# A planned two-layer attention kernel: score banks counted free a little sooner, projections due on two slopes, and all due steps set anew

## The chip, the cores and the metric

The kernel runs on one core of one Trainium2 chip. The metric is the device time of one execution in microseconds. Before the change the median of three runs is 3295.56 us (3295.05 to 3298.42).

## The reference

The input is x, 8 images of 64 x 64 positions with 256 channels, in float32. Two layers follow each other.

Layer 0 projects to q and k (`qkv = x @ w_qkv + b_qkv`, and v is k). The first 128 channels attend inside horizontal windows of 8 x 64 positions, the other 128 inside vertical windows of 64 x 8; every window has 512 positions and 4 heads of 32 channels. A depthwise 3 x 3 convolution of hard_swish(v) is added, and the result goes through hard_swish and an output projection:

```
context = concat(ch, cv)                      # the two kinds of windows
context = hard_swish(context + depthwise3x3(hard_swish(v)) + dw_bias)
return context @ w_out + b_out
```

Layer 1 attends over all 4096 positions of an image with 32 channels: f, g, h are projections with spectrally normalized weights.

```
s = einsum('bnd,bmd->bnm', g, f); beta = softmax(s)
v = einsum('bnm,bmd->bnd', beta, h)
out = gamma * (v @ kv + bv) + x
```

## The kernel before, in words

**Steps.** All 8 images are one stream of 960 steps. A step is a group of score matmuls (s, for 128 keys by 512 queries in each of four row groups of the array), the exponentials of these on ScalarE (ACT, `p<-s`), and later a group of value matmuls (num) that multiply the exponentials into the sum of values. An image has three kinds of units: eight `h` units (horizontal windows) of 4 steps; eight `v` units (vertical windows) of 3 steps, of which the second and the third have three passes of scores instead of two (they share 8 slots of keys in unequal parts, PASSES); and two `l` units (the global attention of layer 1) of 32 steps each, called L0 and L1 below. The first `h` unit of the next image stands ahead of the `l` units of the current one, so that it covers the handover. In PE's program the order is scores of step n, then values of step n - 1, with other PE work before or behind the values.

**Banks.** The scores use three pairs of PSUM banks in turn (`pairs`, two pairs a step), one bank collects the values, and one bank alone (`ps_mm`, one buffer) takes everything else: the projections of q and k (`project`, pq), the projections to f, g (`project_fg`, pf) and h (`project_h`, phd), its transposition (`turn_h`, ph) and the row sums (`sums`). So the next of these can begin only when the one before has been evicted by ACT.

**Filler.** A projection is four pieces (`product_pieces`, HALVES and two halves of the contraction), each 16 matmuls of 128 x 256. There are four projections for each of 8 blocks i of an image: m = 0 and 2 give q and k of the horizontal windows ("near", evicted to qh and kh), m = 1 and 3 those of the vertical windows ("far", evicted to qv, and to kn and kv). Near projections of blocks 1 to 4 (INSIDE) and all far ones of the next image are due while the `l` units of the image before run; `inside_due` spreads them. The exponentials of `l` units are added up by VectorE (DVE, `acc_l`), but the last of four rows is added by DMAs that GpSimd (POOL) issues (`gather`, acc_l and row_l alternately). Convolution taps, hard_swish, normalization and transposes are DVE's and ACT's other work; `clip` and `join` work on a block each. Values of v units go through DRAM (`kt` is written to `kvia` and fetched to `vs` by SyncE's queue, SP).

**The planner.** The order of everything is worked out while the program is built, by the class Flow (lines 90 to 294). Every piece of work is a Task with its engine, an assumed length, what it needs, and a step at which it is due, all from DUE (lines 49 to 55) and the unit's own first step. `step` (line 231) places the scores, then urgent work, the held values of the step before, ACT's evictions (`fill_act`), filler on PE (`fill_pe`), DVE's work (`fill_dve`), and last what SP and POOL issue. It keeps a clock for each engine with its assumed durations. `banks` (line 162) says when the planner takes a pair of banks for free, as the end of the first exponential of the step before plus a lag less a fixed lead; `fill_pe` uses it as the time up to which filler is free, and `late` as the limit of what ACT may take on. A task whose due step has come is placed even if this delays the scores. `require` forces work that a step can't begin without. Since the engines then run in this order, each waits on the chip only for real dependences.

What the prediction's steps touch: `project` (L306 is the matmul's line in `product`), the evictions qh L634, qv L637, kh L649, kn L652 and kv L653, the clips L672 and L904, the first tap on ACT L704 and the other eight on DVE L708, the sums L859 and their copy L580, the copies of num L871 and L1052, `project_h` L956 with its eviction L964 and `turn_h` L970.

Of the kernel before, what the change touches and what calls it, by code (L numbers as in the profile page):

```python
# [21 lines left out]
TB = 512  # L22
NB = N // TB
# [17 lines left out]
def side(h):  # L41
    return slice(h * TB // 2, (h + 1) * TB // 2)
# [4 lines left out]
SLOTS = 8  # L47

DUE = dict(
    near_k=-4, near_q=0, near_values=-25, clip=0, swish=-2, conv_h0=51, conv_h1=13, conv_h2=38,  # L50
    conv_h3=23, conv_v0=-9, conv_v1=20, conv_v2=7, conv_v3=13, tap=-9, join_h=28, join_hl=17, join_v=-8,
    context=19, norm=3, release=-38, sums=8, add=-6, adds_h=1, adds_v=0, group_h=0, group_v=1, add2=-25,
    apart=6, fg0=-12, fg2=28, fg3=31, h0=3, h1=12, values_v=-33, near0=17, spread0=26, spread1=71,
    conv_first=0, far_swish=-33,
)
INSIDE = 4
AHEAD = 16
# [4 lines left out]
SCORES, VALUES, PROD, TURN, DRAIN, PASS, THIRD = 0.96, 0.88, 0.86, 0.65, 0.11, 0.43, 0.5  # L62
EXP, EVICT, COPY, VIEW = 0.97, 0.62, 0.52, 0.42
ADD, ADD3, NORM, SWISH, TAP, TAPS = 2.36, 1.83, 2.5, 0.75, 0.75, 1.28
GATHER, SUMMED = 0.9, 2.6
PE_LAG, LAG, SLACK = 0.28, 0.1, 0.3
ISSUE, LOAD, VIA, FETCH, HALO, BEHIND = 0.6, 4.3, 2.6, 2.8, 0.6, 3.0


# [20 lines left out]
class Flow:  # L90
# [70 lines left out]

    def banks(self):

        end = self.half_end + LAG - DRAIN
        return max(end, self.exp_end + LAG - DRAIN - THIRD) if self.third else end

    def late(self, end):
# [142 lines left out]
def tile_attention_blocks(  # L310
# [18 lines left out]
    nc = tc.nc  # L329
# [98 lines left out]
    sums = prep.tile([P, NF + C + 1], F32, name="sums")  # L428
# [31 lines left out]
    total = check.tile([1, 1], F32, name="total")  # L460
# [13 lines left out]
    def attention(images, load_x, out_rows, exact):  # L474
# [127 lines left out]
        def image(b):  # L602
# [136 lines left out]
            def window_unit(kind, i):  # L739
                nm = f"{b}_{'hv'[kind]}{i}"  # L740
                u = {}
                passes = PASSES if not exact and DUE["group_v" if kind else "group_h"] else {}
                adds = not exact and DUE["adds_v" if kind else "adds_h"]
                if passes:
                    terms = [(2, None)] if adds else [(2, None), ("mid", 1)]
                else:
                    terms = [(3, None)] if adds else [(2, None), (3, 0), (3, 1)]
                terms += [("acc", 0), ("acc", 1)]

                def maxima():  # L750
# [82 lines left out]
                def add(c):  # L833
# [2 lines left out]
                        u["acc"] = work.tile([P, NQ, TB], F32, tag="acc", name=f"acc_{nm}", bufs=1)  # L836
                    nc.vector.tensor_add(u["acc"], u["acc"] if c == 2 else u[0], u[c])  # L837

                def add_mid(c):

                    h = passes[c][0][1]
                    acc = u["acc"].rearrange("p (j i) c -> p i j c", j=2)[:, :, :, side(h)]
                    mid = u["mid", c].rearrange("p i (j c) -> p i j c", j=2)
                    nc.vector.tensor_add(acc, acc, mid)
# [61 lines left out]
                def context():  # L906
# [2 lines left out]
                    nc.vector.scalar_tensor_tensor(a, u["ctx"], 6.0, a, ALU.min, ALU.mult)  # L909

                return SimpleNamespace(
                    steps=3 if passes else 4, passes=passes, terms=terms, adds=adds,
                    scores=scores, weighted=weighted, add=add, add_mid=add_mid, sums=sums,
                    release=release, norm=norm, fetch=fetch, join=join,
                    clip=clip, context=context,
# [219 lines left out]
        flow = Flow()  # L1135
# [33 lines left out]
        readers, last_mids = defaultdict(list), {}  # L1169
# [13 lines left out]
        for u in units:  # L1183
            if not u.kind:
                continue
            e = u.t + u.steps
            w = [weights_ready(u.t + c) for c in range(u.steps)]
            if u.kind == "l":
                chain = None
                for c in range(1, u.steps):  # L1190
                    task = flow.add(
                        "dve", [(partial(u.add, c), [("dve", ADD if exact else ADD3)])], u.t + c + DUE["add"],
                        [w[c]] + ([w[0]] if c == 1 else [chain]), ready=u.t + c + 1,
                    )
                    if c == 1:
                        in_turn("acc", task)
                        readers[u.t].append(task)
                    readers[u.t + c].append(task)
                    chain = task
                gathered = []  # L1200
                for c in range(0 if exact else u.steps):
                    task = flow.add(
                        "rows", [(partial(u.gather, c), [("pool", GATHER), ("dma", SUMMED)])], u.t + c,
                        [w[c], *gathered[-2:-1]], ready=u.t + c + 1,
                    )
                    if c < 2:
                        task.after += last_users["acc"][-1:]
                    readers[u.t + c].append(task)
                    gathered.append(task)
                total = flow.add(  # L1210
                    "pe", [(u.sums, [("pe", PROD * (1 if exact else 1.5)), ("act", COPY)])], e + 1,
                    [chain, *gathered[-2:]], ready=e, bank=True,
                )
                in_turn("sum", total)
                last_users["acc"].append(total)
            else:
                pieces = [(partial(u.add, 1), [("dve", ADD)])]
                if u.passes:
                    pieces.append((partial(u.add_mid, 1), [("dve", TAPS)]))
                acc = pair = flow.add("dve", pieces, u.t + 2, w[:2], ready=u.t + 2)  # L1220
                in_turn("acc", acc)
                if u.adds:
                    add, took = (u.add_mid, TAPS) if u.passes else (u.add, ADD)
                    acc = flow.add(
                        "dve", [(partial(add, 2), [("dve", took)])], u.t + DUE["add2"],
                        [acc, w[2]], ready=u.t + 3,
                    )
                last = len(u.terms) - 1
                pieces = [
                    (  # L1230
                        partial(u.sums, n),
                        [("pe", PROD if h is None else PROD / 2), *([("act", COPY)] if n == last else [])],
                    )
                    for n, (_, h) in enumerate(u.terms)
                ]
                total = flow.add("pe", pieces, e, [acc, *w[2:]], ready=e, bank=True)
                total.then = (last, e + DUE["sums"])
                in_turn("sum", total)
                last_users["acc"].append(total)
                if u.passes:  # L1240
                    held = [(total, last)]
                else:
                    held = [acc if u.adds else (total, last), (total, 2)]
                first = (pair, 1) if u.passes else pair
                for c, task in enumerate((first, first, *held)):
                    readers[u.t + c].append(task)
                if u.passes:
                    last_mids[u.t + 1] = pair
                    last_mids[u.t + 2] = (total, 2) if acc is pair else acc
            u.released = flow.add("act", [(u.release, [("act", COPY)])], e + DUE["release"], ready=e)  # L1250
            shuffle = [("sp", ISSUE), ("dma", VIA)] if u.kind == "v" else []
            u.released.ends = True
            u.total = total
            u.normed = flow.add(
                "dve", [(u.norm, [("dve", NORM), *shuffle])], e + DUE["norm"], [total, u.released], ready=e
            )
            last_users["sum"].append(u.normed)
            u.fetched = u.normed
            if u.kind == "v":
                u.fetched = flow.add("sp", [(u.fetch, [("sp", 4 * ISSUE), ("dma", FETCH)])], e, [u.normed])  # L1260
# [27 lines left out]
        def inside_due(i, far):  # L1288

            n = i + min(i, INSIDE) + far  # L1290
            return DUE["spread0"] + (DUE["spread1"] - DUE["spread0"]) * n // (NB + INSIDE)

        for n, im in enumerate(ims):
            last = ims[n - 1] if n else None
# [3 lines left out]
            for i in range(NB):  # L1298
                u = h[i]
# [5 lines left out]
                ready = start if inside else last.v[0].t + DUE["near0"] if last else max(0, u.t - 4)  # L1305
                if i >= QH:
                    ready = max(ready, h[i - QH].t + u.steps)
# [15 lines left out]
                for m in (1, 3):  # L1323
                    after = [sw[i - 1, 1]] if m == 3 and i else []
                    ready, due = (start, start + inside_due(i, 1)) if last else (0, u.t + 1)
                    end = (("act", 2 * (VIEW if m == 1 else EVICT)),)
# [46 lines left out]
            context = {}  # L1373
# [85 lines left out]
        for u in units:  # L1459
            for c in range(u.steps if u.kind else 0):  # L1460
                n = u.t + c
# [46 lines left out]
        with tc.manual_schedule():  # L1508
            last = None
            steps = [(u, c) for u in units for c in range(u.steps)]  # L1510
            passes = [3 if u.kind in ("h", "v") and c in u.passes else 2 for u, c in steps] + [2]
# [93 lines left out]
```

## Time and profile before

| | |
|---|---|
| median of three runs | 3295.56 us |
| profiled execution | 3301.26 us, its span 3299.4 us |
| mean granted TensorE clock | 0.995 |
| PE busy | 98% of the span |
| DVE busy, ACT busy | 81%, 81% |
| POOL busy | 15% |
| exponentials of two-pass steps (L560) | 1664 of 1025 ns, 1612.6 us |
| adds of l units on DVE (L1037) | 480 of 1758 ns, 843.6 us |
| DMA, mean | 104 GB/s |

Each row of a group gives busy time, the mean of one instruction, and the idle time of the engine before it with what ended that. In a timeline the columns are the start in us, the length in us, engine, line, operation, tiles, shapes and count; `[... <- ...]` is the idle time before it and what released it. Lengths of merged rows reach from the first start to the last end. PE's matmuls overlap and their ends are modelled, so for PE the distance between the starts of neighbouring rows says more than the lengths. The first image takes about the first 300 us up to its `l` units, a middle image some 403 us, and the last image's `l` units, beside which no next image is projected, the last 200 us.

### The profile page before, as it was taken

Reading aid. Unit: us, or ns where it says so; the run is one execution under the profiler, and the core shown is the slowest. Engines: PE = TensorE matmul, PEld = TensorE weight load, DVE = VectorE, ACT = ScalarE, POOL = GpSimd, SP = SyncE. Lnnn points to the kernel's source line nnn. Section 1 sums busy time; section 2 is a strip of 40 time slices with the busy share of each in tenths; the row PEclk is TensorE's granted clock in tenths of the full one; section 3 lists DMA queues with packets and bytes.
Section 4 is the critical chain, followed back from the end, with each engine's and each line's share of the span. In section 5 each row is a group of like instructions: output and inputs, shape, how many; then the busy total and the mean of one; then the engine's idle time right before and its main releaser. Section 6 shows DMA issues by size and latency. Waiting matters only on the chain. (4 is left out here: it accounts for less than half of the span.)

```text
span 3299.4 us, 83480 instructions
## 1 busy us (share of the span) xinstructions
PE 3244.3 (98%) x35348; PEld 1182.5 (36%) x35348; DVE 2662.0 (81%) x2404; ACT 2663.4 (81%) x3235; POOL 510.8 (15%) x776
## 2 busy tenths in 40 slices
PE   7899999999999999999999999999999999999998
PEld 2344233432334323353333533334333342334422
DVE  4899688986899759997698976989769987689864
ACT  5688787887878878888788887788877888778876
POOL 0001230012200222002220022200321003210132
PEclk9999999999999999999999999999999999999999
DMA  2124652256523565235542365423654236532465
GB/s 73 48 83 117 124 123 91 77 127 125 110 91 86 122 130 112 82 87 123 128 107 80 101 119 125 103 78 104 124 130 100 78 101 130 125 102 65 104 128 110
DMA packets 321118, 344.41 MB, mean 104 GB/s; under 512 B 34272, under 2 KB 198624, under 8 KB 320736
## 3 DMA queue, kind: packets, MB, share of 16 engines
q0 software_dynamic: 71680, 134.25, 23.1%
q1 hardware_dynamic: 246816, 204.18, 20.8%
q8 instruction: 280, 4.59, 0.6%
q10 hardware_dynamic: 2240, 0.56, 0.1%
q14 instruction: 102, 0.84, 0.1%
HBM read 99.78 MB, written 83.89 MB: 56 GB/s over the span
## 5 line engine op out<-in xcount | busy, mean ns | idle before, releaser
L560 ACT ACTIVATE p<-s 128x1024 f32<-128x1024 f32 x1664 | 1612.6, 1025 | 226.7 <-PE s L1006 149.6
L1037 DVE TENSOR_TENSOR acc_l<-acc_l,p 128x1536 f32<-128x1536 f32 x480 | 843.6, 1758 | 350.6 <-ACT p L560 346.8
L708 DVE SCALAR_TENSOR_TENSOR act<-hv,dw_sb,act 128x1024 f32<-128x1024 f32 x512 | 653.0, 1279 | 18.0 <-ACT act L704 7.9
L1006 PE MATMUL s<-gq,f 32*128 32x512 f32 x4096 | 606.3, 640 | 4.3 <-ACT p L560 4.0
L306 PE MATMUL pq<-x,wqkv_sb 128*32 128x256 f32 x8192 | 540.3, 384 | 8.5 <-ACT kv L653 6.4
L1022 PE MATMUL num_l<-p,h_sb 128*32 128x512 f32 x4096 | 545.5, 605 | 0.3 <-ACT nums_l L1052 0.3
L306 PEld LDWEIGHTS pq<-x,wqkv_sb 128*32 128x32 f32 x8192 | 267.2, 111 | 393.1 <-issue 243.0
L799 PE MATMUL s<-qh,kh 32*128 32x512 f32 x2048 | 299.0, 640 | 6.4 <-ACT qh L634 5.6
L1048 POOL DMA_DIRECT2D row_l<-p x240 | 211.4, 881 | 507.6 <-ACT p L560 494.4
L828 PE MATMUL num_h<-p,vs 128*32 128x512 f32 x2048 | 273.3, 606 | 8.0 <-ACT nums_h L871 4.4
L1048 POOL DMA_DIRECT2D acc_l<-p x240 | 210.9, 879 | 426.0 <-ACT p L560 371.3
L1006 PEld LDWEIGHTS s<-gq,f 32*128 32x128 f32 x4096 | 173.6, 182 | 279.9 <-issue 264.0
L306 PE MATMUL s<-act,wout_sb 128*32 128x512 f32 x2048 | 227.6, 594 | 0.2 <-ACT ot_l L1115 0.2
L775 PE MATMUL s<-qv,kv 32*128 32x256 f32 x3072 | 218.8, 397 | 0.2 <-ACT p L793 0.2
L1022 PEld LDWEIGHTS num_l<-p,h_sb 128*32 128x32 f32 x4096 | 80.7, 108 | 384.3 <-issue 371.3
L1088 ACT ACTIVATE ot_l<-s,bias_o 128x512 f32<-128x512 f32 x120 | 76.2, 684 | 163.3 <-PE s L306 152.1
L821 PE MATMUL num_v<-p,vs 128*32 128x256 f32 x3072 | 194.0, 386 | 0.0
L775 PEld LDWEIGHTS s<-qv,kv 32*128 32x128 f32 x3072 | 146.5, 185 | 81.6 <-issue 57.9
L788 ACT ACTIVATE p<-s 128x1024 f32<-128x1024 f32 x128 | 131.5, 1027 | 44.0 <-PE s L775 44.0
L687 POOL MEMSET hv<- 128x18 f32 x64 | 20.6, 322 | 924.0 <-ACT sum_sb_v L580 712.5
L837 DVE TENSOR_TENSOR acc_v<-p 128x2048 f32<-128x2048 f32 x64 | 146.5, 2288 | 17.6 <-PE sum_h L859 7.8
L837 DVE TENSOR_TENSOR acc_h<-p 128x2048 f32<-128x2048 f32 x64 | 145.9, 2279 | 14.0 <-ACT p L560 12.8
(140 smaller groups left out, 3197.6 us busy)
## 6 DMA issues: line engine op xcount, KB each, us to landing
acc_l<-p POOLq DMA_DIRECT2D x256, 256.0 KB, 3.4
row_l<-p POOLq DMA_DIRECT2D x256, 256.0 KB, 3.3
x<-in_xT SPq DMA_DIRECT2D x92, 512.0 KB, 4.1
kvia<-kt SPq DMA_DIRECT2D x128, 256.0 KB, 2.5
vs<-kvia SPq DMA_DIRECT2D x512, 64.0 KB, 2.0
out<-ot_l SPq DMA_DIRECT2D x128, 256.0 KB, 2.1
via_v<-nums_v SPq DMA_DIRECT2D x64, 256.0 KB, 2.0
shuf_v<-via_v SPq DMA_DIRECT2D x256, 64.0 KB, 2.1
```

Source lines behind the costliest of these rows:

```text
L306: nc.tensor.matmul(out[quad(r), :], lhsT=lhsT[:, quad(r)], rhs=rhs, start=start, stop=stop)
L560: nc.scalar.activation(pt[:, 2 * z : 2 * z + 2, :], sc[z], AF.Exp, scale=scale)
L708: nc.vector.scalar_tensor_tensor(o, src, wt, o, ALU.mult, ALU.add)
L775: mm = nc.tensor.matmul(place_of(n, r, h, sc), lhsT=k[quad(r), t * P : (t + 1) * P], rhs=q[quad(r), side(h)], start=True, stop=True,)
L799: nc.tensor.matmul(row_of(sc, r), lhsT=k[quad(r), c * P : (c + 1) * P], rhs=q[quad(r), :], start=True, stop=not exact,)
L821: nc.tensor.matmul(u["num"][quad(r), side(h)], lhsT=vs[kind, i][:, r, t, :], rhs=place_of(n, r, h, (pt[:, :2], u["mid", c], pt[:, 2:])), s ...
L828: nc.tensor.matmul(u["num"][quad(r), :], lhsT=vs[kind, i][:, r, c, :], rhs=u[c][:, r, :], start=(c == 0), stop=(c == 3),)
L837: nc.vector.tensor_add(u["acc"], u["acc"] if c == 2 else u[0], u[c])
L1006: nc.tensor.matmul(row_of(sc, r), lhsT=f4[quad(r), c * P : (c + 1) * P], rhs=gq[quad(r), z, :], start=True, stop=not exact,)
L1022: nc.tensor.matmul(u["num"][quad(r), :], lhsT=h_sb[:, c, :], rhs=u[c][:, r, :], start=(c == 0), stop=(c == 4 * NB - 1),)
L1037: nc.vector.tensor_add(acc, u[0][:, :rows, :] if c == 1 else acc, u[c][:, :rows, :])
L1048: nc.gpsimd.dma_start(out=u["row", c % 2], in_=u[c][:, rows, :], accum_op=ALU.add)
```

## The change

It has four parts.

1. `banks` counts the score banks free 0.16 us sooner (the new constant EARLY).
2. `inside_due` goes through three points, spread0, spread_mid and spread1, instead of through two: one slope up to the blocks INSIDE, another from there on.
3. All due steps in DUE are other numbers; spread_mid and add3 are new.
4. Further adds of exponentials on DVE in place of row-sum matmuls can be asked for (`extra`, `add_more`); how many are made is set by adds_h and adds_v, which stay at 1 and 0.

```diff
 DUE = dict(
-    near_k=-4, near_q=0, near_values=-25, clip=0, swish=-2, conv_h0=51, conv_h1=13, conv_h2=38,
-    conv_h3=23, conv_v0=-9, conv_v1=20, conv_v2=7, conv_v3=13, tap=-9, join_h=28, join_hl=17, join_v=-8,
-    context=19, norm=3, release=-38, sums=8, add=-6, adds_h=1, adds_v=0, group_h=0, group_v=1, add2=-25,
-    apart=6, fg0=-12, fg2=28, fg3=31, h0=3, h1=12, values_v=-33, near0=17, spread0=26, spread1=71,
-    conv_first=0, far_swish=-33,
+    near_k=-7, near_q=-2, near_values=-50, clip=42, swish=21, conv_h0=106, conv_h1=18, conv_h2=27,
+    conv_h3=36, conv_v0=65, conv_v1=13, conv_v2=32, conv_v3=27, tap=-21, join_h=-53, join_hl=28,
+    join_v=12, context=-28, norm=14, release=-34, sums=-18, add=48, adds_h=1, adds_v=0, group_h=0,
+    group_v=1, add2=12, add3=98, apart=8, fg0=-7, fg2=-15, fg3=3, h0=36, h1=7, values_v=-102, near0=-69,
+    spread0=14, spread1=66, spread_mid=68, conv_first=80, far_swish=-20,
 )
...
-PE_LAG, LAG, SLACK = 0.28, 0.1, 0.3
+PE_LAG, LAG, SLACK, EARLY = 0.28, 0.1, 0.3, 0.16
...
-        end = self.half_end + LAG - DRAIN
+        end = self.half_end + LAG - DRAIN - EARLY
...
-                if passes:
-                    terms = [(2, None)] if adds else [(2, None), ("mid", 1)]
-                else:
-                    terms = [(3, None)] if adds else [(2, None), (3, 0), (3, 1)]
+                last = 2 if passes else 3
+                extra = [("mid", 2) if passes else ("all", 2), (0, last), (1, last)][:adds]
+                terms = [(last, None), (last, 1), ()][max(0, adds - 1)]
+                terms = [terms] if terms else []
+                if not adds:
+                    terms = [(2, None), ("mid", 1)] if passes else [(2, None), (3, 0), (3, 1)]
...
+                def add_more(what, c):
+
+                    if what == "mid":
+                        return add_mid(c)
+                    cols = slice(0, TB) if what == "all" else side(what)
+                    acc = u["acc"][:, :, cols]
+                    nc.vector.tensor_add(acc, acc, u[c][:, :, cols])
...
-            return DUE["spread0"] + (DUE["spread1"] - DUE["spread0"]) * n // (NB + INSIDE)
+            first, mid, last = DUE["spread0"], DUE["spread_mid"], DUE["spread1"]
+            if n <= 2 * INSIDE + 1:
+                return first + (mid - first) * n // (2 * INSIDE + 1)
+            return mid + (last - mid) * (n - 2 * INSIDE - 1) // (NB - INSIDE - 1)
```

The tasks that call `add_more` replace the one that called `add` or `add_mid` for the third step of a unit, and the lists of readers that free the slots of the exponentials name them.

More of the change, by code (lines that the diff above doesn't have):

```diff
@@ L911, in window_unit @@
                 return SimpleNamespace(
-                    steps=3 if passes else 4, passes=passes, terms=terms, adds=adds,
+                    steps=3 if passes else 4, passes=passes, terms=terms, extra=extra, add_more=add_more,
                     scores=scores, weighted=weighted, add=add, add_mid=add_mid, sums=sums,
@@ L1221, in attention @@
                 in_turn("acc", acc)
[L1222 to L1226, printed above, removed]
+                mores = {}
+                for what, c in u.extra:
+                    acc = mores[what] = flow.add(
+                        "dve", [(partial(u.add_more, what, c), [("dve", ADD if what == "all" else TAPS)])],
+                        u.t + (DUE["add2"] if c == 2 and what in ("mid", "all") else DUE["add3"]),
+                        [acc, w[c]], ready=u.t + c + 1,
                     )
@@ L1239, in attention @@
                 last_users["acc"].append(total)
[L1240 to L1243, printed above, removed]
+                final = mores.get(1) or (total, last if u.passes or u.extra else 2)
+                held = [final] if u.passes else [mores.get("all") or (total, last), final]
                 first = (pair, 1) if u.passes else pair
@@ L1248, in attention @@
                     last_mids[u.t + 1] = pair
-                    last_mids[u.t + 2] = (total, 2) if acc is pair else acc
+                    last_mids[u.t + 2] = mores.get("mid") or (total, 2)
             u.released = flow.add("act", [(u.release, [("act", COPY)])], e + DUE["release"], ready=e)
```

## The prediction, made before the changed kernel ran

> **What bounds the kernel now.** I read the page's busy times first, then the waits of PE, then PE's timeline step by step, since every step starts at a score matmul (s).
>
> ```profile
> PE 3244.3 (98%) x35348; PEld 1182.5 (36%) x35348; DVE 2662.0 (81%) x2404; ACT 2663.4 (81%) x3235; POOL 510.8 (15%) x776
> ```
>
> PE bounds the kernel, but its ends are modelled, so I take the distance from one start to the next. A step of the global attention with one piece of filler (pq), at 1955 us, and steps with none, in the last image:
>
> ```profile
> 1955.04 1.14 PE L1006 MATMUL s<-gq,f 32*128 32x512 f32 x8
> 1956.11 1.06 PE L1022 MATMUL num_l<-p,h_sb 128*32 128x512 f32 x8
> 1957.00 0.61 PE L306 MATMUL pq<-x,wqkv_sb 128*32 128x256 f32 x8
> 1957.54 1.14 PE L1006 MATMUL s<-gq,f 32*128 32x512 f32 x8
> ```
> ```profile
> 3155.77 1.34 PE L1006 MATMUL s<-gq,f 32*128 32x512 f32 x8
> 3157.04 1.06 PE L1022 MATMUL num_l<-p,h_sb 128*32 128x512 f32 x8
> 3158.03 1.14 PE L1006 MATMUL s<-gq,f 32*128 32x512 f32 x8
> 3159.10 1.06 PE L1022 MATMUL num_l<-p,h_sb 128*32 128x512 f32 x8
> 3160.10 1.31 PE L1006 MATMUL s<-gq,f 32*128 32x512 f32 x8
> ```
>
> Scores take 1.07 to the next start, values 0.88 before a filler and 0.99 before scores, a piece 0.43 plus 0.12 before scores: 2.50 with one piece, 2.06 with none. So a piece costs 0.44 wherever it stands; PE's floor doesn't depend on the order. What does are waits. In the second fence every other scores group takes 1.27 or 1.24 instead of 1.07: its second half waits for a bank that the exponentials (ACT, two of 1.02 us a step) still read. **A step without filler costs 0.18 in every second of a row, also when it stands alone** (1984.59 to 1985.83 is such a one). Summing step by step what exceeds these floors gives about 99 us of waits: 36 in the first image (H 23.4, V 9.9, L 2.5), 7.4 in each of images 1 to 6 (one has 8.5), 17 in the last. More than that can't be won; the six middle images, the bulk of the time, run at 98% of their floor.
>
> Two further kinds of wait:
>
> ```profile
> 57.17 1.91 PE L306 MATMUL pq<-x,wqkv_sb 128*32 128x256 f32 x32
> 60.46 1.93 PE L306 MATMUL pq<-x,wqkv_sb 128*32 128x256 f32 x32 [1.39 <-ACT kv L653]
> 63.21 1.14 PE L799 MATMUL s<-qh,kh 32*128 32x512 f32 x8 [0.81 <-ACT qh L634]
> ```
> ```profile
> 3096.85 0.61 PE L956 MATMUL phd<-act,wcomb 128*32 128x256 f32 x8
> 3099.36 0.66 PE L970 MATMUL ph<-ident,h 128*128 128x128 f32 x4 [1.89 <-ACT h L964]
> 3101.51 2.64 PE L821 MATMUL num_v<-p,vs 128*32 128x256 f32 x24
> ```
> ```profile
> core 0: us, PE busy (x) PEld busy (x) DVE busy (x) ACT busy (x) POOL busy (x), PEclk, DMA share, GB/s
> 3100.50:3103.80 3.30, 3.30 (x32) 0.99 (x24) 3.18 (x5) 2.08 (x3) 0.00 (x0) 0.50 0.21 79
> ```
>
> First: two projections back to back share the one bank, so the second waits for the first's evictions (1.39) and the scores for the second's (0.81). Second: after an idle stretch of 1.89 us the granted clock is 0.50 for some 3.4 us, and the values matmuls take 2.64 where others take 1.50.
>
> **The change, part by part.** The built order has the same number of instructions on every engine before and after (PE 17709, ACT 3248, DVE 2405); the new branches for further adds stay unused with these settings. Only places move. So I count places in the order and price them by the rows above. PE's runs fall from 2707 to 2583; each insertion of filler costs 0.007 (0.88+0.44+0.12 against 0.99+0.43): **-0.8**.
>
> *Middle images (six).* Pieces of filler and steps without any, in one image:
> L0 35 pieces, 4 empty steps -> 35, 19; L1 60, 2 -> 53, 6; H 37, 7 -> 52, 3; V 20, 11 -> 12, 13. L0 now does five projections in whole blocks of four pieces first (block step 3.79; ACT 1.94 for the exponentials plus 0.7 to 2.1 of evictions and clips, which fits) and then runs nearly bare. DVE follows: 1.76 per add in 2.15.
> - L0 (steps 0 to 31 of l): bare runs of 9, 1, 1 and 8 steps (10 to 18, 20, 22, 24 to 31) give 5+1+1+4 = 11 waits of 0.175 = 1.9, against two (0.35) before: +1.55.
> - L1: bare steps 43, 54-55, 62-63. The last pair follows evictions of kn and kv (0.58 apart), about 0.45; in all 0.8 against 0.17: +0.6.
> - End of L0: a num copy, kn, kv and a clip in one go make scores wait 1.76 (1989 to 1994 us); the clip (0.61 to the next start on ACT) moves behind the sums: -0.6.
> - First L step: the f piece now stands between scores and values, where 0.37 was waited: -0.37.
> - H's tail, four bare steps and two more, waited 0.88; two pieces go into each but the last: -0.7.
> - V: its wait of 0.28 per window (the third exponential) is in the same places; clips after a num copy fit into ACT's idle 0.43, after a sum copy they cost 0.26; two first convolution taps (ACT, act<-hv, 1.25) no longer stand before or beside a sum copy (0.4 each): about 0. The handover to L: +0.1.
> Sum **+0.6 each, +3.6 for six**. Bounds: -1 (bare steps free when alone, V's waits halved) to +2 each.
>
> *First image.* Four back-to-back pairs (57.17, 76.53, 95.90, 117.69) wait 2.47 three times and 4.89 once, 12.3 in all; six other waits (1.47, 2.16, 1.61, 0.88) 6.1. In the new order each pair is split by a values group (0.97): the first's evictions end about 0.73 after it, the scores still wait for qh: 1.6 each, 6.4. One more such pair (1.2), a row sum behind a projection (1.6) and a projection behind a row sum (1.4) are new; the combined weights are followed by values instead of a projection, 0.8 (0 to 1.5: whether the clock drops there). 18.4 -> 11.4: **-7.0** (bounds -11, with only qh's 0.81 per pair, and -3, with the old 2.47).
> V's first values wait for their transposed k by way of DRAM: 2.9 in the trace, 10.65 after the last far projection. That projection is now one step later, so the cover shrinks by 2.4; a store that stood in SP's queue ahead of this fetch now stands behind it (1.2 sooner): a wait of 4.15. Two such first taps that cost 1.65 later are gone. **-0.5** (-3 to +3). Here the Trainium skill's "TensorE: Matmul & The Clock Gate", section "Why this matters for your kernels", says that only idle gaps over about 3 us bring the clock back to half. The rows say less suffices: 2.20 us at 97.8, 1.89 at 3097.5. By the page the old wait of 2.9 costs no clock and the new one of 4.15 does, +3 more; by the rows both pay (the trace has 0.50 from 189.0 to 195.6). I take the rows.
> Its L0: 12 bare steps and two later runs: **+0.7**.
>
> *Last image.* The h projection is whole, and a clip no longer stands before its eviction: the wait of 2.05 before ph falls to about 1: -1.1. By the page the clock stayed up anyway; by the row it dropped (1.64), and a gap of 1 us is below any that did it: -1.6. Two clips fewer in the first bare steps, -0.8; two clips in bare steps that had a piece, +0.8. **-2.7**.
>
> Sum: -0.8+3.6-7.0-0.5+0.7-2.7 = **-6.7 us**. The profiled execution took 3301.26 (span 3299.4), which is 5.7 over the median; 3301.26 would become 3294.6, and the median of the runs 3295.56 becomes **3288.9**.
>
> **Rivals.**
> 1. *More is won* (3278): the waits are fewer than the order shows, since ACT arrives at each bare run freer than before and V's 0.28 and 0.6 shrink with it. For: ACT's 173 us in the 207 of H and V leave room. Against: the 1.24 repeats in bare runs where ACT has nothing else. At -1 per middle image instead of +0.6: 10 us less.
> 2. *It cancels* (3296): the pairs of the first image wait as before (2.47, +3.5), and the bare runs' evictions cost twice what I took (+0.6 each, +3.6): -6.7+7.1. For: L0's 19 bare steps are certain, the gains are estimates.
> 3. *Slower, the row gathers* (3312): POOL adds each step's last row by DMA, and each must land before the next but one. Two bare steps give 4.31 us; the landing has median 3.3 and maximum 6.2, and POOL waited 29.2 us for it (15 times). From a mean landing over 4.31 in the bare run it sets the pace: 4.6 means 0.15 a step, over 22 steps of seven images 23 us. Against: 20 bare steps of the last image kept 4.31, with POOL waiting for ACT alone.
> That the change does nothing is excluded by the order.
>
> **How the numbers follow.** Forecast 0.50 (own range 3284 to 3294), more won 0.20, cancels 0.22, slower 0.08. 0.2% is 6.6 us, about what a measurement can tell from no change; the forecast sits on that bound, and I put 0.32 of its 0.50 beyond it, as its new pairs were priced with every eviction in full. Faster 0.32+0.20 = 0.52; same 0.18+0.20 = 0.38; slower 0.02+0.08 = 0.10. The range 3277 to 3299 reaches over both neighbours and leaves out the gathers.
>
> **What would show it.** Right: L0 of middle images with scores alternating 1.07 and 1.24; no start-to-start of 6.04 for 64 matmuls in the first 130 us, but gaps of 0.7 before a projection; 0.50 clock only once between 100 and 3290 us, at V's start; each middle image longer by about 0.6. Wrong: POOL's gathers waiting for DMA in L0; middle images shorter by over 1 us, or waits of DVE on H and V's sums; PE instruction counts other than before.

## The result, and the profile after

| | kernel before | kernel after |
|---|---|---|
| median of the runs | 3295.79 us (20 runs, 3291.81 to 3301.07) | 3293.28 us (20 runs, 3289.73 to 3295.92) |
| ratio, with its 95% interval | | 0.9991 (0.9984 to 0.9998) |
| a second set of runs beside each other | 3295.94 us (30 runs) | 3293.09 us (13 runs), 0.9992 (0.9983 to 1.0000) |
| profiled execution, span | 3301.26, 3299.4 us | 3294.10, 3292.3 us |

The change wins 2.5 us, 0.09%: within the 0.2% that the prediction called no change, where it had put 0.38. The forecast of 3288.9 was 4.4 us too low; the result lies at the upper end of its own range (3284 to 3294). The profile's busy times hardly differ from those before:

```profile
PE 3244.5 (99%) x35348; PEld 1191.2 (36%) x35348; DVE 2666.3 (81%) x2404; ACT 2667.3 (81%) x3235; POOL 513.4 (16%) x776
```

So again only waits can have changed. (A piece of filler is 4 matmuls, 8 rows of the trace, and a projection 16 and 32; the account of the kernel above gives the projection's number to the piece. The step times are not touched by it. After the change the lines from L799 on are 2 higher, those behind L839 10 or more.) Three places of PE's timeline carry the result. First, the pair of projections that stood at 57.17 us:

```profile
52.99 1.14 PE L801 MATMUL s<-qh,kh 32*128 32x512 f32 x8
54.06 1.93 PE L306 MATMUL pq<-x,wqkv_sb 128*32 128x256 f32 x32
55.81 1.04 PE L830 MATMUL num_h<-p,vs 128*32 128x512 f32 x8
57.38 1.93 PE L306 MATMUL pq<-x,wqkv_sb 128*32 128x256 f32 x32 [0.53 <-ACT kv L653]
60.12 1.14 PE L801 MATMUL s<-qh,kh 32*128 32x512 f32 x8 [0.81 <-ACT qh L634]
```

The values group stands between the two, and the idle time in front of the second falls from 1.39 to 0.53; the 0.81 for qh stays. By the floors (the prediction's start-to-start distances without waits) this step now runs 1.59 over, where it ran 2.47 over before; 1.6 was predicted. Second, a bare run in L0 of a middle image:

```profile
1933.57 1.14 PE L1016 MATMUL s<-gq,f 32*128 32x512 f32 x8
1934.64 1.06 PE L1032 MATMUL num_l<-p,h_sb 128*32 128x512 f32 x8
1935.63 1.34 PE L1016 MATMUL s<-gq,f 32*128 32x512 f32 x8
1936.90 1.07 PE L1032 MATMUL num_l<-p,h_sb 128*32 128x512 f32 x8
```

Scores take 1.07 and 1.27 to the next start in turn, and exactly 11 such waits come in each L0, as counted. Third, the last image, with the same place as the rows at 3096.85 before:

```profile
3088.62 0.66 PE L980 MATMUL ph<-ident,h 128*128 128x128 f32 x4 [0.81 <-ACT h L974]
3089.21 1.13 PE L1016 MATMUL s<-gq,f 32*128 32x512 f32 x6
3092.07 2.04 PE L1016 MATMUL s<-gq,f 32*128 32x512 f32 x2 [1.73 <-DMA gq<-fg]
3094.04 2.36 PE L823 MATMUL num_v<-p,vs 128*32 128x256 f32 x20
```
```profile
3091.80:3095.20 3.40, 3.13 (x14) 1.09 (x18) 3.29 (x4) 0.99 (x1) 0.00 (x0) 0.50 0.36 118
3095.20:3098.60 3.40, 3.40 (x24) 0.91 (x16) 0.85 (x1) 0.62 (x2) 0.00 (x0) 0.50 0.12 27
```

(In the second fence the columns are those of the table of stretches in the prediction: PE, PEld, DVE, ACT, POOL busy, then the granted clock.) The wait before ph has fallen from 1.89 to 0.81, as the prediction had it. But the first global scores now wait 1.73 for a DMA, gq, that nobody had waited for, and behind that idle stretch the clock is 0.50 for 6.8 us instead of 3.4. SP's queue says why:

```profile
3084.32 2.41 SPq L956 DMA_DIRECT2D f<-fg  x4
3086.77 0.59 SPq L957 DMA_DIRECT2D gq<-fg  x1
3087.41 2.49 SPq L956 DMA_DIRECT2D f<-fg  x4
3089.94 0.59 SPq L957 DMA_DIRECT2D gq<-fg  x1
```

The projection f7.1 is at step 893 instead of 892, and its ten transfers are issued one by one, the second gq last of all, 5.6 us after the first. It landed 2.0 us later, at 3092; the scores stood ready at 3090. In the kernel before, the last gq was issued at 3096.25 and landed as quickly, 1.7 us ahead of the first global scores:

```profile
3096.25 0.59 SPq L947 DMA_DIRECT2D gq<-fg  x1
3099.94 1.64 PE L1006 MATMUL s<-gq,f 32*128 32x512 f32 x8
```

In a middle image seven steps lie between the f projection (f4.1) and the first global scores.

**Where the time went.** From the first scores to those of the last step, the three profiles of the kernel before (two are experiments below) take 3242.2 us on average, the two of the kernel after 3237.7: 4.5 less. By image, from first scores to first scores 120 steps later:

| | first image | images 1 to 6, undisturbed | images 1 to 6, together | last image |
|---|---|---|---|---|
| before (mean of three) | 450.6 | 402.8 | 2418.6 | 373.0 |
| after (mean of two) | 441.9 | 403.2 | 2419.3 | 376.4 |
| after, gq first (mean of two, below) | 440.2 | 403.2 | 2419.3 | 370.6 |

The first stretch holds one projection (32 rows, 1.8 us) fewer than before and the last one more. With that set right the first image wins 6.9 us and the last loses 1.6.

### The profile page after: what moved, and what is told of

It is laid out like the page before. It is cut to its first block, busy times and chain, and to the rows that moved or that the text cites. A ratio compares the mean times of both kernels' runs of the same rounds, so it can differ in the third digit from the quotient of the medians.

```text
span 3292.3 us, 83473 instructions
## 1 busy us (share of the span) xinstructions
PE 3244.5 (99%) x35348; PEld 1191.2 (36%) x35348; DVE 2666.3 (81%) x2404; ACT 2667.3 (81%) x3235; POOL 513.4 (16%) x776
## 5 line engine op out<-in xcount | busy, mean ns | idle before, releaser
L1016 PE MATMUL s<-gq,f 32*128 32x512 f32 x4096 | 618.3, 641 | 1.7 <-DMA gq<-fg 1.7
L306 PE MATMUL pq<-x,wqkv_sb 128*32 128x256 f32 x8192 | 516.1, 381 | 4.4 <-ACT kv L653 2.1
L1016 PEld LDWEIGHTS s<-gq,f 32*128 32x128 f32 x4096 | 187.1, 183 | 332.4 <-issue 323.7
L1058 POOL DMA_DIRECT2D acc_l<-p x240 | 210.5, 877 | 426.7 <-ACT p L560 332.3
L839 DVE TENSOR_TENSOR acc_h<-p 128x2048 f32<-128x2048 f32 x64 | 146.3, 2285 | 53.5 <-PE sum_h L869 48.0
L1056 POOL DMA_DIRECT2D acc_l<-p x16 | 9.2, 577 | 1145.0 <-PE sum_h L869 961.5
L839 DVE TENSOR_TENSOR acc_v<-p 128x2048 f32<-128x2048 f32 x64 | 146.6, 2291 | 21.0 <-PE sum_h L869 9.8
```

Of the source, the lines that this page charges most:

```text
L306: nc.tensor.matmul(out[quad(r), :], lhsT=lhsT[:, quad(r)], rhs=rhs, start=start, stop=stop)
L1016: nc.tensor.matmul(row_of(sc, r), lhsT=f4[quad(r), c * P : (c + 1) * P], rhs=gq[quad(r), z, :], start=True, stop=not exact,)
L1058: nc.gpsimd.dma_start(out=u["row", c % 2], in_=u[c][:, rows, :], accum_op=ALU.add)
```

## The experiments

**The kernel before, once more.** No edit.

> The kernel before, unchanged, for a second profile. Theory: waits step by step agree with the first profile within 0.2 us wherever the granted clock is full; what differs between executions is at which of the idle stretches of 1.3 to 3 us the clock falls to 0.50 (3.4 or 6.8 us each, costing 1.6 to 3). So the profiled time may lie anywhere in 3291 to 3301 and the ratio is 1.000 within its interval (about 0.0007 wide to each side). Rival: the clock drops at 97.8-100, 144, 189 and 3100 us belong to the program and all come again at the same places; then the first profile's 3301 against the median of 3295.6 has another cause.

Measured: 3295.14 us, ratio 1.0001 (0.9992 to 1.0009). Undisturbed middle images agree to 0.1 us. Apart from one near 28 us and one at the end, which both profiles have, the stretches at clock 0.50 were, by the trace's record of the clock, at 100.1, 144.5, 188.9 (6.83 us long) and 3100.5 in the first profile, and at 100.6 (6.83 us) and 145.0 in this one, with none at V's start or at the first global scores of the last image: the same idle stretches are there, but not all drop the clock. Every such stretch in every profile is 3.41 or 6.83 us long, but for the one that the program's end cuts off. This cost or spared a place up to some 3 us (V's second and third steps take 11.40 together in the first profile and 8.21 in this one).

The runs of these kernels, sorted by their mean granted clock, show how far this spreads the runs of one kernel (mean times in us; the five at 0.995 and 0.999 are left out; the first column has the runs of the edit of SP's queue on the kernel before too, which changes nothing, see below):

| mean granted clock | before | after | after, gq first |
|---|---|---|---|
| 0.998 | 3293.71 (41 runs) | | 3286.18 (8) |
| 0.997 | 3296.11 (56) | 3291.37 (13) | 3287.01 (5) |
| 0.996 | 3298.84 (13) | 3294.16 (17) | 3289.55 (5) |
| mean clock of all | 0.99725 | 0.99630 | 0.99717 |

At equal clock the kernel after is 4.7 us faster, about the number that the profiles gave (4.5). Its clock is lower by 0.00095, and a step of 0.001 costs 2.4 to 2.8 in the first two columns, so some 2.4 us go back: 4.7 - 2.4 = 2.3, against 2.5 and 2.9 measured.

**gq's transfers first** (the kernel after):

```diff
             def fetch_fg(p):
                 t = part["fgt", p]
                 for i in (2 * p, 2 * p + 1):
                     z = i % 2 * 2
+                    nc.sync.dma_start(out=gq[quad(i % NQ), i // NQ, :], in_=t[quad(z + 1)])
+                for i in (2 * p, 2 * p + 1):
+                    z = i % 2 * 2
                     for r in range(NQ):
                         nc.sync.dma_start(out=f4[quad(r), i * TB : (i + 1) * TB], in_=t[quad(z)])
-                    nc.sync.dma_start(out=gq[quad(i % NQ), i // NQ, :], in_=t[quad(z + 1)])
```

> The kernel after with the two gq transfers of a block of f issued ahead of its eight f4 transfers instead of among them; the order on every engine but SP stays. Theory: in the last image the wait of 1.73 us of the first global scores for gq and the stretch at clock 0.50 behind it (about 3.3 us) go: 3293.3 becomes 3288.3 (3286.5 to 3291); nothing else changes. Rival 1: the f4 transfers, now later, are waited for in their place, or ph's wait of 0.81 alone drops the clock: 3291.5 to 3294. Rival 2: the wait of the profile was peculiar to that execution: no change.

Measured: 3286.10 us, 0.9971 (0.9960 to 0.9981) of the kernel before. And once more, beside the kernel after:

> The kernel after with gq's transfers first, once more, beside the kernel after on the same chip. Theory: 3286.1 within 1.5 us, 6 to 8 us below the kernel after: 1.73 of wait, about 3.4 of half-speed clock behind it, and the values group that stood in the window. Rival: the earlier 7 us held chance, and it is 5 or less.

> The kernel after, unchanged, once more. Theory: 3293.3 within 1 us, and in its profile again the wait of 1.7 to 1.8 for gq in the last image with a half-speed window behind it; its mean granted clock is about 0.001 below that of the kernel before, and at equal granted clock it is 4 to 5 us faster than the kernel before. Rival (the gain of 2.5 was chance): within 1 us of the kernel before, and no difference at equal clock.

Measured: 3288.73, 0.9975 (0.9966 to 0.9985), and 3293.09, 0.9992 (0.9983 to 1.0000). By the ratios the late gq costs 6.6 and 5.6 us, in the pooled medians (3287.3 against 3293.2) 5.9; the table of clocks gives 4.4 to 4.6 at equal clock and some 2.2 by the clock. The repeat's own medians are 4.4 apart, which is its rival's number and not its theory's 6 to 8, so the size is known to some 2 us only; that it is there is not in doubt, since the wait is in both profiles of the kernel after and in neither of the other. In the second profile of the kernel after it is longer than the 1.7 to 1.8 that was expected, and the clock is again at 0.50 for 6.83 us behind it:

```profile
3094.53 2.04 PE L1016 MATMUL s<-gq,f 32*128 32x512 f32 x2 [2.10 <-DMA gq<-fg]
```

The timeline of the second profile with gq first:

```profile
3090.24 0.66 PE L982 MATMUL ph<-ident,h 128*128 128x128 f32 x4 [0.81 <-ACT h L976]
3090.83 1.14 PE L1018 MATMUL s<-gq,f 32*128 32x512 f32 x8
```
```profile
3086.37 1.15 SPq L955 DMA_DIRECT2D gq<-fg  x2
3087.57 5.02 SPq L959 DMA_DIRECT2D f<-fg  x8
```

The scores follow at once, the clock stays up, and the f transfers that now come last are waited for by nobody. Both versions of the kernel are beaten by this one.

**The same edit on the kernel before.**

> The kernel before with the same edit of SP's queue that took 7 us from the kernel after: the two gq transfers of a block of f ahead of its f4 transfers. Theory (the wait for gq in the last image is made by the change, which puts the projection f7.1 one step later; before, the transfers landed in time): no change, 3294.8 within 1.5 us, and the last image's L keeps its 8.5 to 10 us of waits. Rival (the late gq costs the kernel before as well, hidden in another row of its trace): 2 us or more faster, and then the edit says nothing about the change.

Measured: 3294.72, 0.9997 (0.9988 to 1.0005). The order of the transfers costs the kernel before nothing: the late gq is made by the change.

**The first image's pairs alone** (the kernel before; one condition in the due step of near projections):

```diff
-                        (u.t + DUE["near_k" if m else "near_q"]) if due is None else due, [], after, ready, True,
+                        (u.t + (DUE["near_k"] - (0 if last else 3) if m else DUE["near_q"] - (0 if last else 2))) if due is None else due, [], after, ready, True,
```

> The kernel before with one thing of the change: in the first image alone the near projections are due 3 (k) and 2 (q) earlier, which splits its back-to-back pairs by a values group; all later images keep the order of before, instruction for instruction. Theory (the gain of the change is these pairs): the first image's H loses 5 to 7 us of waits, the pairs' steps 1.6 each as after the change; the middle images stay at 7.4 us of waits each; 3295.8 becomes about 3289.8 (3287.5 to 3292), ratio 0.9975 to 0.999, and faster than the whole change. Rival (the gain lies in the middle images or in the counting of banks): within 2 us of before, 3294 to 3298.

Measured: 3300.25, 1.0016 (1.0009 to 1.0022): slower, and the theory's number failed by 10 us. Its mechanism was there, each pair's step at 1.59. But the planner put everything behind the pairs elsewhere too. A row sum moved ahead of a values group (4.5 us over the floor at step 21); at step 25 a values group waited 3.27 for ACT's copy of num, and the clock was down for 6.83 us (5.3 over the floor, 1.6 before); and in L0 five small pieces of ACT's work came together:

```profile
317.61 1.33 ACT L904 ACTIVATE shuf_v<-act,three 128x512 f32<-128x512 f32 x2
...
319.98 0.73 ACT L672 ACTIVATE hv<-kn,three 128x512 f32<-128x512 f32 x1
320.59 3.77 ACT L560 ACTIVATE p<-s 128x1024 f32<-128x1024 f32 x4
```
```profile
319.18 1.13 PE L1006 MATMUL s<-gq,f 32*128 32x512 f32 x4
321.67 1.13 PE L1006 MATMUL s<-gq,f 32*128 32x512 f32 x4 [1.37 <-ACT p L560]
```

3 us of small work on ACT between two exponentials make half of the next scores wait: the step runs 4.2 us over its floor, 2.5 of them in the scores and 1.7 by the clock drop that followed (at 323.2). The run's mean clock was 0.9958.

**The first image's pairs undone** (the kernel after, the opposite edit: `+ (0 if last else 3)` and `+ (0 if last else 2)`):

> The kernel after with the first image's near projections due as before (k 3, q 2 later); the middle and the last image keep the order of after. Back-to-back pairs stand again in steps 7, 11 and 15. Theory: each of the three waits 2.47 instead of 1.59, +2.6 us, and half-speed clock windows behind their idle stretches make it +3 to +7: 3296.5 (3294.5 to 3300). Rival (after the experiment on the kernel before, which lost in its middle what its pairs won: the pairs' waits are made up elsewhere): 3293.3 within 1.5 us.

Measured: 3304.36, 1.0029 (1.0019 to 1.0040), 11 us above the kernel after and above the range that was given (to 3300). All of it lies in the first image (453.1 us from first scores to first scores, against 441.9). The three pairs wait 2.47, 2.46 and 2.47, as expected; the larger part was not. V's first values:

```profile
PE num_v L830 <- DMA vs<-kvia: 8.7, 1, 8.7
PE num_v L830 <- DMA vs<-kvia: 3.1, 1, 3.1
```

(The upper row is this run's, the lower the kernel after's, both from PE's waits.) A projection for the next image stood ahead of the last far one, its eviction and a clip ahead of that one's evictions on ACT, and three taps ahead of the transposition of kv on DVE.

So both runs confirm the price of a pair (2.47 unsplit, 1.59 split), but neither shows what the pairs are worth to the whole: the planner moved other work in both. The first image's gain below is therefore read from the rows of the traces, not isolated by a run.

**Parts of the change.** The count of banks undone (`EARLY = 0.0` in the kernel after), the count alone (`- 0.16` in the kernel before), the second slope undone (`spread_mid=53` in the kernel after).

> The kernel after with the planner's 0.16 of earlier free banks taken back to 0, all due steps and both slopes kept. The first image's H and the last image's projections keep the order of after; in the middle images L0 has its 19 bare steps in one run (9 or 10 waits of 0.175 instead of 11), H 1 bare instead of 3, V 14 bare. Theory (the due steps carry the result): 3293.3 within 1.5 us; first image's H at 16 us of waits; middle images within 0.5 each of after. Rival (the earlier count carries the gain): back at the kernel before, 3295.5 to 3297, with waits of the first image's H above 20.

> The kernel before with the earlier count of free banks alone (0.16 us), all due steps and the one slope as before. By its order the first image keeps its unsplit pairs, L0 of the middle images 4 bare steps, V 6 bare instead of 11 and 16 pieces instead of 20, and f7.1 goes one step later, ahead of a values group. Theory: this part alone wins nothing, since the count only moves places and the due steps were set for another count: 3293.5 to 3300. Rival (it is the part that wins): 3291 or less, with the middle images' waits below 6.5 us each.

> The kernel after with one slope for the projections ahead, as before (their middle point 53 instead of 68), all else kept. By its order L0 has 14 bare steps instead of 19 (7 waits of 0.175 instead of 11), H 12 bare instead of 3, V 14 bare and 8 pieces, the first image's pairs split as after; f7.1 moves to step 895, just ahead of the global scores that need it. Theory: the wait for gq in the last image grows from 1.73 to some 6 us and pays for a half-speed window too, +5; V of the middle images waits for its exponentials as in the run without the earlier count, +1 to +2 each: 3304 (3297 to 3312). Rival (the slopes decide nothing but L0's bare steps): 3292 to 3294.

Measured: 3318.16, 1.0067 (1.0053 to 1.0081); 3403.84, 1.0329 (1.0315 to 1.0344); 3378.37, 1.0255 (1.0241 to 1.0269). Each of them is slower than both kernels, by 23 to 109 us against the kernel before and outside of what theory and rival gave: neither "the due steps carry the result" nor "this part wins" is right. Without the count, middle images took 406.2 us instead of 403.2, in two ways. The clip `nums_h` moved from behind a num copy to behind a third exponential:

```profile
1815.84 1.03 ACT L795 ACTIVATE p<-s 128x1024 f32<-128x1024 f32 x1
1816.75 0.73 ACT L914 ACTIVATE nums_h<-act,three 128x512 f32<-128x512 f32 x1
1817.36 1.95 ACT L560 ACTIVATE p<-s 128x1024 f32<-128x1024 f32 x2
```
```profile
1818.50 2.00 PE L777 MATMUL s<-qv,kv 32*128 32x256 f32 x24
1820.42 1.07 PE L830 MATMUL num_v<-p,vs 128*32 128x512 f32 x8
```

The two exponentials end 0.6 later, and the scores of three passes take 1.92 to the next start instead of 1.51; three of these, with 0.45 and 0.19 in two more steps, make 1.9 us an image. The other is the handover from V to L, which the last experiment below takes alone. In the run of the count alone V's exponentials wait for their buffers, which DVE's adds free (one such row below); that its due steps were set for another count is the likely reason, but is not shown:

```profile
1849.16 1.94 ACT L560 ACTIVATE p<-s 128x1024 f32<-128x1024 f32 x2 [3.06 <-DVE acc_v L837]
```

Its V scores waited 43 us for ACT in 57 places, and middle images took 410 to 420 us. With one slope they took 413, by some 10 more us of waits in H. The first global scores of the last image waited 2.0 for gq, hardly more than after the change, where some 6 had been expected; with the clock down their step ran 6.5 over its floor (5.1 after the change), and the last image took 394.4 us instead of 376.4.

**Half of the count** (gq first, `EARLY = 0.08`):

> The kernel after with gq's transfers first and 0.08 instead of 0.16 in the count of free banks. In the middle images only the handover from V to L moves by its order: f4.1 and the h projection go one to two steps later, so that the transposition of h stands beside V's last sum; V's clips stay where they were, and the first image's H is unchanged. Theory (without the earlier count, 25 us were lost, by the handover about 1.1 us an image and by clips behind third exponentials in V about 1.9): the handover alone costs about 1.1 in each of seven images, 3286.1 becomes 3294 (3290.5 to 3296). Rival (V's clips cost all of the 3 us an image): 3286.1 within 1.5.

Measured: 3296.69 us, 8 us above the kernel with gq first on the same chip, just outside the range that was given (to 3296). Middle images take 404.5 us, 1.3 more, of which the ten steps around the handover have 1.2; 1.1 was expected. The wait is the one expected, 1.0 in six images:

```profile
PE sum_v L869 <- ACT h_sb L983: 6.2, 6, 1.3
```

So a step's delay of the h projection makes ph stand next to V's last row sum, and both need the one bank that ACT must first evict.

## Why the prediction was right and wrong

| step of the sum | predicted | measured |
|---|---|---|
| first image: H | -7.0 | -8.7 |
| first image: V | -0.5 | +2.0 |
| first image: L0 | +0.7 | -0.2 |
| six middle images, with insertions | +2.8 | +0.7 together; +2.4 where undisturbed |
| last image | -2.7 | +1.6; -4.2 with gq first |
| sum | -6.7 | -4.6 in the profiles (-4.7 at equal clock) |
| mean granted clock | not counted | +2.4 |

- **First image.** Right in sum (-6.8 against -6.9), but by luck: three misses cancel. The four pairs were priced within 0.01, and the three new waits nearly so: 1.2, 1.6 and 1.4 on paper, 1.17, 1.60 and 1.71 in the run. The row sum behind a projection, for one, starts 3.35 after it, where a projection in front of values takes 1.75:

```profile
125.19 1.91 PE L306 MATMUL pq<-x,wqkv_sb 128*32 128x256 f32 x32
128.54 1.06 PE L869 MATMUL sum_h<-p,ones 128*32 128x512 f32 x8 [1.45 <-ACT kv L653]
```

H won more because the combined weights cost less: before, they took 1.44 and 2.19 and their projection 4.00 to the next starts; after, 1.44 and 1.41, with no projection behind. That wins 3.0, where the prediction's 2.16 against 0.8 is 1.4. V went the other way: its waits grew by 2.0 (mean of two profiles against three, the row sum that moved from V to L, 2.15, set right). The first values waited 3.12 and not 4.15. But in the first profile a row sum then waited 1.8 for `acc_v`, whose adds stood behind five taps of a convolution on DVE (6.6 us from 177.5); and in both, four steps on, an exponential waited 2.1 for the next such add, and the clock dropped behind it. The prediction read DVE's average of 81% and its two-pass adds in L, not its queue at V's start; waits of DVE on V's sums were among its own signs of being wrong.
- **Middle images.** Right in sign and close in size: +0.40 each against some +0.5. L0's waits came out as counted. (The price of 0.007 for an insertion does not follow from the rounded figures beside it, which give 0.02, but it fits the rows: 2.50 and 3.79 for steps with one piece and with four.)
- **Last image.** This is the step that failed: -2.7 was predicted and +1.6 measured. The prediction followed the h projection and its clips, and the wait before ph fell as said; but it did not follow the f projection, which is one step later. Its ten transfers in SP's queue were the thing to check: the last issue starts 5.6 us after the first, and the first global scores come three steps after the projection. The rule that every issued instruction of a moved step counts was kept for V's stores and left out here.
- **The clock.** "By the page the old wait of 2.9 costs no clock and the new one of 4.15 does, +3 more; by the rows both pay": neither is the rule. The wait at V's start was 3.12 in the kernel after without a drop, and 3.24 in the run with gq first with one; the two rows below are of these two, in this order. The Trainium skill's "TensorE: Matmul & The Clock Gate", section "What's actually happening", describes windows of 4096 cycles (3413 ns) that run freely and don't start with the kernel. The traces agree: all stretches at 0.50 are 3.41 or 6.83 us long, and within a profile all changes of the clock lie on one grid of 3.41 us, whose place in the program differs from profile to profile. On this grid 1.95 us of the wait of 3.12 fell into one window, and 2.91 of the wait of 3.24; the last section has all such waits. So I had read a stable price into one execution. The 1.6 us for the end of a drop in the last image stood in two of the three profiles of the kernel before. Of the signs that the prediction named, the clock at 0.50 only once between 100 and 3290 us did not come: leaving out the program's end, it was so twice and three times in the two profiles of the kernel after.

```profile
178.79 1.07 PE L830 MATMUL num_v<-p,vs 128*32 128x512 f32 x8 [3.12 <-DMA vs<-kvia]
```
```profile
177.83 1.94 PE L830 MATMUL num_v<-p,vs 128*32 128x512 f32 x8 [3.24 <-DMA vs<-kvia]
```

- **Carrying the sum to the median.** The profile of before was 5.5 us above the median of its runs, which the prediction saw and carried over as a plain difference. Its three profiles have mean clocks of 0.995, 0.996 and 0.997 against 0.99725 of the runs: such executions hold more drops, and a part of their waits is not there in the median.
- **The rivals.** "It cancels" came nearest in time (3296), but its mechanism did not occur: the pairs no longer wait 2.47, and the bare runs' evictions do not cost twice as much. "More is won" missed that a new wait had been made. "The row gathers" fell as to time, though its sign came: POOL's waits for the gathers' DMA grew from 52 to 140 us in all (the 29.2 of the prediction is one row of four), but no row of PE's waits names the gathers, and two bare steps still take 4.31 to 4.34.

What stays open: what the first image's parts are worth when nothing else moves, why three profiles of the kernel before all have a lower clock than its mean run, and how large the cost of gq's wait is to better than 2 us.

## What to carry to other kernels

When a piece of work moves by even one step, follow all that it issues to the one who waits for it, the last transfer of a series above all, and issue first what is needed first: that order was worth more than the whole change. The settings of a planner are a set: here leaving one part out, or making one alone, lost 23 to 109 us where the whole won 2.5, so a part's effect is read from the order that it makes, not from its purpose. Before a few microseconds of one profile are priced, take a second one and compare at equal granted clock.

## What the hardware showed

Within each of the thirteen profiles, the changes of the granted clock lie whole multiples of 3.41 us apart (in the kernel after, 26.7 to 204.1 is 52 of them and 204.1 to 3091.8 is 846). Whether an idle PE drops the clock depends on how the idle time falls on these windows. PE's wait for V's first values is nearly the same in eleven profiles, but the largest part of it that lies in one window is not:

| profile | wait, us | largest part in one window | clock behind it |
|---|---|---|---|
| one slope | 3.29 | 3.03 | 0.50 |
| gq first, both | 3.24, 3.22 | 2.91, 2.57 | 0.50 |
| after, second | 3.21 | 2.43 | 0.50 |
| before, first | 2.92 | 2.37 | 0.50 |
| half of the count | 3.09 | 2.18 | 0.50 |
| count alone | 2.78 | 1.97 | 0.50 |
| after, first | 3.12 | 1.95 | 1.00 |
| count undone | 3.17 | 1.81 | 1.00 |
| before with gq first | 2.72 | 1.42 | 1.00 |
| before, second | 2.69 | 1.35 | 1.00 |

The wait of 1.89 in the last image before the change did the same: whole in one window it dropped the clock (two profiles), split into 0.42 and 1.47 it did not. Idle time alone is not the whole rule, since other windows with 1.2 to 1.9 us of it went both ways. The parts are worked out from the starts and ends of the waits and the grid; PE's ends are modelled, so 0.02 between two rows says nothing.

The drops go with much of the spread of 4 to 10 us between runs of one kernel: mean clock and time correlate with -0.70 (the 112 runs of the first column of clocks above) and -0.82 (33 of the kernel after), and 0.001 of mean clock is worth 2.4 to 2.8 us. The first step's scores start at either 19.9 to 20.7 or 21.9 to 22.2 us in the thirteen profiles, whatever the kernel.
